# Squared context norms added on ScalarE, and two roundings placed behind the zero point

## The chip, the cores and the metric

The kernel runs on one core of one Trainium2 chip. Its time is the device time of one execution, in microseconds (us). The program has four layers, one after the other, and is written in a framework that takes instructions in program order and lets a planner set the order of each engine's queue. The engines are named as in the profile: PE (TensorE), DVE (VectorE), ACT (ScalarE), POOL (GpSimd) and SP (the queue that starts most transfers).

## The reference

There are 32 sequences of 128 tokens with 128 features, and a context of the same shape. Layer 1 is a gated attention over the context. Layer 2 is a dense layer in quantised arithmetic, 128 to 512 to 128. Layer 3 aligns each context sequence with its token sequence by dynamic time warping. Layer 4 is a mixture of eight experts. The change touches the second half of layer 2 and the start of layer 3:

```
def _affine_quantize(x):
    amin, amax = (jnp.min(x), jnp.max(x))
    scale = jnp.maximum((amax - amin) / 255.0, 1e-08)
    zp = jnp.clip(jnp.round(-amin / scale) + QMIN, QMIN, QMAX)
    q = jnp.clip(jnp.round(x / scale) + zp, QMIN, QMAX)
    return (q, scale, zp)
...
def _qlinear(x, W, b):
    xq, sx, zx = _affine_quantize(x)
    wq, sw = _sym_quantize(W)
    acc = jnp.einsum('bsh,oh->bso', xq - zx, wq)
    return acc * (sx * sw) + b
...
def _pairwise_euclidean(a, b):
    aa = jnp.sum(a * a, axis=-1)[:, None]
    bb = jnp.sum(b * b, axis=-1)[None, :]
    ab = a @ b.T
    return jnp.sqrt(jnp.maximum(aa + bb - 2.0 * ab, 0.0))
...
x = x + jnp.tanh(g_ffn[0]) * _L0_ffn_ref(_layernorm(x, axis=-1), L0_ffn_W1, L0_ffn_b1, L0_ffn_W2, L0_ffn_b2)
x = x + jnp.tanh(g_xattn[1]) * _L1_xattn_ref(ctx_1024, _layernorm(x, axis=-1))
```

In the distances `a` is the context and `b` the normalised tokens.

## The kernel before

The sequences are taken in eight groups of four (`GB` is 4, `NG` is 8). Tokens lie in `X`, 128 tokens on the partitions, and the hidden values of the dense layer in `HT`, hidden features on the partitions.

**The scale and the zero point.** After the first matmul and the GELU of layer 2, VectorE reduces `HT` to one maximum and one minimum (L819, L820, L837), and `max_everywhere` spreads them over the partitions. `affine_scale` then works out, in instructions of one element a partition, the scale (L234, L235), its reciprocal `inv` (L237) and from it the zero point: L239 to L242 each need the one before, and L244 and L246 make `lo` and `hi` of it. `lowest` turns `lo` into the two columns of `low` (L764, L765). The product of the two scales, `s2`, is made on the side by two instructions (L851, L853).

**The second dense layer.** `dense(n)`, for each of eight blocks of 512 columns of `HT`:

- VectorE multiplies by `inv` and rounds to whole numbers by adding a large constant (L865). It needs `inv` but not the zero point.
- ScalarE subtracts the lower bound and cuts at zero with a Relu (L868). It needs `low`.
- VectorE cuts at 255 and adds the lower bound (L869).
- TensorE multiplies by the second weight, sixteen matmuls a block (L874).
- VectorE scales by `s2` and adds to `X` (L879).

The list `ties` sets an order on VectorE: the rounding of block n is queued behind `ties[n]`. For blocks 0 and 1 that is the last multiplication of `s2` (L853), and for block n from 2 on it is L869 of block n - 2.

**The distances.** After every second block, `norm_steps` normalises two groups: statistics (L147 and after), an inverse root by iteration (L174 to L182), the normalised rows `y` (L203), and their transposes on TensorE (L207). Its steps are laid between the steps of the next two blocks, three at a time. For each group `take(g, tp)` follows:

- ScalarE writes minus two times the transposed rows, and their squares (L884, L886).
- TensorE makes squared norms of the tokens minus two times the products with the context, in one bank `d2` (L888, L890).
- For each of the four sequences the squared norm of the context, one number a partition in `aa[:, b]`, is added and the sum cut at zero (L897, on VectorE). `aa` is made by L793, L848 and L849 before the scale is known.
- ScalarE takes the square root in two halves of the partitions, the second with its columns reversed (L901, L902).
- Two transfers write the halves to `d_dram` (L904), from SP's queue; the last of all goes from ScalarE's.

Layer 3 starts with loads from `d_dram` (L978), and its rows (L993, L994) run on VectorE. POOL fills its borders before (L983 and after).

Of the kernel before, what the change touches and what calls it, by code (L numbers as in the profile page):

```python
# [12 lines left out]
AF = mybir.ActivationFunctionType  # L13
ALU = mybir.AluOpType
# [17 lines left out]
MAGIC = 12582912.0  # L32
# [6 lines left out]
def tile_flamingo_gated(  # L39
# [21 lines left out]
    nc = tc.nc  # L61

    def pool(stack, name, bufs=1, space=None):
        kw = {} if space is None else {"space": space}
        return stack.enter_context(tc.tile_pool(name=name, bufs=bufs, **kw))

    def new(p, shape, dt, tag, bufs=None):
        kw = {} if bufs is None else {"bufs": bufs}
        return p.tile(shape, dt, tag=tag, name=tag, **kw)
# [67 lines left out]
    tgf = new(keep, [P, 2], F32, "tgf")  # L137
# [47 lines left out]
    def norm_steps(p, psp, s0, n, take, tag, shape=None):  # L185

        xq = X[:, s0 : s0 + n, :]
        m, w = (8, "") if n <= 8 else (16, "_w")
        mean = new(p, [P, m], F32, "bn_mean" + w)[:, 0:n]
        r = new(p, [P, m], F32, "bn_r" + w)[:, 0:n]  # L190
        for _ in row_norm_steps(p, xq, n, mean, r):
            yield
        for h in range(n // GB):
            if shape is None:
                tp = new(psp, [P, GB, S], F32, tag)
            else:
                if h % 2 == 0:
                    pair = new(psp, shape, F32, tag)
                tp = pair[:, h % 2]
            for i in range(GB):  # L200
                j = GB * h + i
                y = new(p, [P, D], F32, "y", bufs=6)
                got = nc.vector.tensor_scalar(  # L203
                    y, xq[:, j, :], mean[:, j : j + 1], r[:, j : j + 1], ALU.subtract, ALU.mult
                )
                held["y"] = getattr(got, "ins", got)
                nc.tensor.transpose(tp[:, i, :], y, ident)  # L207
                if i % 2 == 1:
                    yield
            take(s0 // GB + h, tp)  # L210
            yield

    def max_everywhere(p, psp, stat, n, tag, share=None):

        if share is None:
            row = new(psp, [n, P], F32, tag + "_row", bufs=1)
            bc = new(psp, [P, n], F32, tag + "_bc", bufs=1)
        else:
            both = new(psp, [P, GB, S], F32, share)
            row, bc = both[0:n, 0, :], both[:, 1, 0:n]  # L220
        nc.tensor.transpose(row, stat, ident)
        red = new(p, [n, 1], F32, tag + "_red")
        nc.vector.tensor_reduce(red, row, AX.X, ALU.max)
        dg = new(p, [n, n], F32, tag + "_dg")
        nc.vector.tensor_scalar(dg, ident[:n, :n], red, None, ALU.mult)
        nc.tensor.matmul(bc, lhsT=ones[:n, :], rhs=dg, start=True, stop=True)
        got = new(p, [P, n], F32, tag)
        nc.vector.tensor_copy(got, bc)
        return got

    def affine_scale(p, mm, tag):

        sc = new(p, [P, 1], F32, tag + "_sc")
        nc.vector.tensor_tensor(sc, mm[:, 0:1], mm[:, 1:2], ALU.add)  # L234
        nc.vector.tensor_scalar(sc, sc, 1.0 / 255.0, 1e-8, ALU.mult, ALU.max)  # L235
        inv = new(p, [P, 1], F32, tag + "_inv")
        nc.vector.reciprocal(inv, sc)  # L237
        zp = new(p, [P, 1], F32, tag + "_zp")
        nc.vector.tensor_scalar(zp, mm[:, 1:2], inv, 300.0, ALU.mult, ALU.min)  # L239
        nc.vector.tensor_scalar(zp, zp, -300.0, MAGIC, ALU.max, ALU.add)  # L240
        nc.vector.tensor_scalar(zp, zp, MAGIC, -128.0, ALU.subtract, ALU.add)
        nc.vector.tensor_scalar(zp, zp, -128.0, 127.0, ALU.max, ALU.min)  # L242
        lo = new(p, [P, 1], F32, tag + "_lo")
        nc.vector.tensor_scalar(lo, zp, -1.0, MAGIC - 128.0, ALU.mult, ALU.add)  # L244
        hi = new(p, [P, 1], F32, tag + "_hi")
        nc.vector.tensor_scalar(hi, zp, -1.0, MAGIC + 127.0, ALU.mult, ALU.add)  # L246
        return sc, inv, lo, hi
# [34 lines left out]
    with ExitStack() as st:  # L282
# [213 lines left out]
        def take(g, tp):  # L496
            nc.scalar.copy(YT[:, GB * g : GB * g + GB, :], tp)
            v = YT[:, GB * g : GB * g + GB, :].rearrange("p b s -> p (b s)")
            nc.vector.tensor_reduce(xst[:, 0, g : g + 1], v, AX.X, ALU.max)
            nc.vector.tensor_reduce(xst[:, 1, g : g + 1], v, AX.X, ALU.min, negate=True)  # L500
# [137 lines left out]
        def finish(s0, n, HN, d2, ms):  # L638
# [30 lines left out]
            for _ in norm_steps(lp, p_at, s0, n, take, "at"):  # L669
                yield  # L670
# [86 lines left out]
    with ExitStack() as st:  # L757
# [3 lines left out]
        def lowest(lo, tag):  # L761

            low = new(fp, [P, 2], F32, tag)
            nc.vector.tensor_scalar(low[:, 1:2], lo, -1.0, None, ALU.mult)  # L764
            nc.vector.tensor_scalar(low[:, 0:1], lo, MAGIC, None, ALU.subtract)  # L765
            return low

        xs2 = new(fp, [P, 2], F32, "xs2")
        nc.vector.tensor_reduce(xs2, xst, AX.X, ALU.max)
        with ExitStack() as st2:  # L770
            fps = pool(st2, "ffnps", space=PSUM)
            mm = max_everywhere(fp, fps, xs2, 2, "mmx")
            sx, inv, lo, hi = affine_scale(fp, mm, "qx")
            s1 = new(fp, [P, 1], F32, "s1")
            nc.vector.tensor_mul(s1, sx, wsc[:, 0:1])
            low_x = lowest(lo, "low_x")
        hst = new(fp, [P, 2, 4 * NC], F32, "hst")
        with ExitStack() as st2:
            xp = pool(st2, "xq")
# [58 lines left out]
        aa = new(fp, [P, B], F32, "aa")  # L838
        with ExitStack() as st2:
            fps = pool(st2, "ffnps2", space=PSUM)  # L840
            mm = max_everywhere(fp, fps, hs2, 2, "mmh")
            sh, inv, lo, hi = affine_scale(fp, mm, "qh")
# [6 lines left out]
            nc.scalar.copy(aa, aa_ps)  # L849
        s2 = new(fp, [P, 1], F32, "s2")  # L850
        nc.vector.tensor_mul(s2, sh, wsc[:, 1:2])  # L851
        low = lowest(lo, "low")
        tie = nc.vector.tensor_mul(s2, s2, tgf[:, 0:1])  # L853
        ties = [tie, tie]


# [25 lines left out]
        def take(g, tp):  # L882
            ym2 = new(dp, [P, GB, S], F32, "ym2")
            nc.scalar.activation(ym2, tp, AF.Copy, scale=-2.0)  # L884
            ysq = new(dp, [P, GB, S], F32, "ysq")
            nc.scalar.activation(ysq, tp, AF.Square)  # L886
            d2 = new(dps, [P, GB, S], F32, "d2")
            nc.tensor.matmul(d2, lhsT=ones, rhs=ysq, start=True, stop=False)  # L888
            for i in range(GB):
                nc.tensor.matmul(  # L890
                    d2[:, i, :], lhsT=CD[:, GB * g + i, :], rhs=ym2[:, i, :],
                    start=False, stop=(i == GB - 1),
                )
            dd = new(dp, [P, GB, S], F32, "dd")
            for i in range(GB):
                b = GB * g + i
                nc.vector.tensor_scalar(  # L897
                    dd[:, i, :], d2[:, i, :], aa[:, b : b + 1], 0.0, ALU.add, ALU.max
                )
            dist = new(dp, [P, GB, S], F32, "dist")  # L900
            nc.scalar.activation(dist[0:SH], dd[0:SH], AF.Sqrt)  # L901
            nc.scalar.activation(dist[SH:P], dd[SH:P, :, ::-1], AF.Sqrt)  # L902
            for h in range(2):
                (nc.sync, nc.scalar if g == NG - 1 else nc.sync)[h].dma_start(  # L904
                    out=d_dram[h, GB * g : GB * g + GB].rearrange("b r j -> r b j"),
                    in_=dist[SH * h : SH * h + SH],
                )
# [335 lines left out]
```

## Time and profile before

| | |
|---|---|
| three runs | 898.74 us median (895.69 to 906.18) |
| profiled execution, time | 896.11 us |
| profiled execution, span | 894.3 us |
| granted TensorE clock, mean over the span | 0.856 |
| busy: PE, DVE, ACT, POOL | 672.0, 555.8, 379.5, 19.3 us |
| first half of layer 2 (176 to 221 us): DVE, ACT busy | 40.58, 34.17 us |
| second half of layer 2 with the distances (221 to 288 us): PE, DVE, ACT busy | 40.84, 52.60, 35.37 us |
| rows of the warping (288 to 372 us): DVE busy | 69.93 us |

The span goes from the first to the last instruction. A row of a window gives each engine's busy time and the number of its instructions. A row of a group gives the line, the engine, the operation, what is written from what, the shape and the count; then the busy time and the mean duration of one in ns; then the engine's idle time just before such instructions and what ended it. A row of the timeline begins with the start and the duration; where several instructions of a kind run together they share a row, and a bracket tells how long the engine had been idle and who released it. L865 is line 865 of the kernel.

### The profile page before, as it was taken

What the parts mean: (1) busy time and instruction counts of PE and PEld (TensorE: products, weight loads), DVE (VectorE), ACT (ScalarE), POOL (GpSimd) and SP (SyncE); (2) the same over time, 40 slices, a digit from 0 to 9 for tenths busy, and PEclk for the clock granted to TensorE, in tenths of its full rate; (3) what the DMA queues carried; (4) which work ended last, traced back from release to release, by engine and by line L of the source; (5) the groups of instructions that cost most, each with busy time, mean ns of one, the idle gap of its engine ahead of it and who ended that gap; (6) DMA issues with size and microseconds to landing.
All of it is one profiled execution on the core that took longest, in us unless ns stands there. A gap on an engine that the chain in (4) does not pass through costs nothing.

```text
span 894.3 us, 12616 instructions
## 1 busy us (share of the span) xinstructions
PE 672.0 (75%) x4682; PEld 454.2 (51%) x4682; DVE 555.8 (62%) x1975; ACT 379.5 (42%) x640; POOL 19.3 (2%) x52
## 2 busy tenths in 40 slices
PE   5789997152475000017999999999999999999997
PEld 2245554110353000005777667777777777777776
DVE  7667999889885799786673556995322333222332
ACT  3796875694464000002443444334433334333342
POOL 2000000004000000000000000000000000000000
PEclk9897998555578555556999999999999999999999
DMA  8000000400012535100000000000000000000000
GB/s 314 33 8 6 2 2 2 188 0 0 1 37 58 126 78 120 42 0 1 1 1 1 1 1 1 12 2 24 1 12 1 1 12 1 12 1 1 12 1 12
DMA packets 11943, 25.32 MB, mean 28 GB/s; under 512 B 2386, under 2 KB 7250, under 8 KB 11090
## 3 DMA queue, kind: packets, MB, share of 16 engines
q1 hardware_dynamic: 9880, 20.19, 7.3%
q10 hardware_dynamic: 1874, 4.23, 2.2%
q8 instruction: 36, 0.59, 0.3%
q14 instruction: 25, 0.20, 0.1%
q0 software_dynamic: 128, 0.10, 0.0%
HBM read 14.01 MB, written 4.46 MB: 21 GB/s over the span
## 4 chain that ended last, share of the span: by engine, by line
PE 52%; DVE 22%; issue 2%; ACT 2%; DMA 1%; DVEq 0%; ACTq 0%; POOLq 0%
PE mpo L1173 25%; PE mph L1164 22%; DVE ru L994 3%; DVE hit L1040 3%; DVE hst L819 2%; DVE hst L820 2%; DVE ru L993 2%; DVE bn L147 1%; PE d L888 1%; PE po L874 1%; PE d L890 1%; PE small L1104 1%; DVE pt L1088 1%; PE px L1091 1%; PE px L1100 1%
## 5 line engine op out<-in xcount | busy, mean ns | idle before, releaser
L1173 PEld LDWEIGHTS mpo<-mw2s,hT 128*128 128x128 f32 x2048 | 252.1, 192 | 62.6 <-issue 39.2
L1167 ACT ACTIVATE hT<-mph,mb1s 128x512 f32<-128x512 f32 x256 | 176.0, 687 | 239.3 <-PE mph L1164 237.6
L1173 PE MATMUL mpo<-mw2s,hT 128*128 128x128 f32 x2048 | 256.4, 276 | 0.1
L1164 PE MATMUL mph<-YT,mw1s 128*128 128x512 f32 x512 | 244.5, 600 | 0.0
L1152 DVE SCALAR_TENSOR_TENSOR X<-mpo,GA,X 128x128 f32<-128x128 f32 x192 | 54.0, 343 | 197.9 <-PE mpo L1173 197.9
L1164 PEld LDWEIGHTS mph<-YT,mw1s 128*128 128x128 f32 x512 | 88.0, 193 | 62.6 <-issue 62.5
L1152 DVE SCALAR_TENSOR_TENSOR X<-mb2s,GA,X 128x128 f32<-128x128 f32 x256 | 73.2, 343 | 0.0
L947 PE MATMUL gt_ps<-ident,ru 32*128 32x32 f32 x1 | 0.3, 281 | 78.7 <-DVE ru L994 78.7
L947 PEld LDWEIGHTS gt_ps<-ident,ru 32*128 32x128 f32 x1 | 0.2, 176 | 78.9 <-issue 78.9
L1030 ACT COPY dv<-vv 128x8 bf16<-128x8 bf16 (+1 forms) x5 | 1.1, 220 | 79.0 <-DVE vv L1026 47.6
L554 ACT ACTIVATE dm<-bi 128x512 f32<-128x512 f32 x48 | 28.8, 602 | 11.3 <-issue 4.2
L994 DVE TENSOR_TENSOR_SCAN ru<-ru,dc 64x128 f32<-64x128 f32 x64 | 26.7, 417 | 5.9 <-DMA dc<-d_dram 3.9
L596 DVE TENSOR_TENSOR sm<-sc,dm 128x512 f32<-128x512 f32 x32 | 21.7, 684 | 12.8 <-ACT dm L554 9.8
L810 PE MATMUL ph<-XQ,w1q 128*128 128x512 bf16 x32 | 15.8, 615 | 17.1 <-DVE XQ L801 9.2
L874 PE MATMUL po<-w2q,hqt 128*128 128x128 bf16 x128 | 12.9, 278 | 17.8 <-DVE hqt L869 17.8
L868 ACT ACTIVATE hqt<-HT,low 128x2048 bf16<-128x2048 f32 x8 | 15.8, 1998 | 24.5 <-DVE low L764 14.9
L1101 ACT COPY YT<-px 128x512 f32<-128x512 f32 x8 | 4.7, 586 | 49.6 <-PE px L1100 49.6
L1046 PE MATMUL vt<-ident,vw 64*64 64x64 f32 x1 | 0.3, 310 | 32.3 <-DVE hit L1040 32.3
L1040 DVE SCALAR_TENSOR_TENSOR hit<-jotab,vw,DV 64x128 bf16<-64x128 bf16 x63 | 21.7, 344 | 4.6 <-DMA DV<-dv 2.4
L1181 ACT COPY ye<-mpo 128x512 f32<-128x512 f32 x16 | 9.4, 586 | 35.2 <-PE small L1118 17.8
L510 ACT ACTIVATE qm<-YT,mcol 128x512 f32<-128x512 f32 x32 | 23.1, 727 | 0.0
L147 DVE BATCH_NORM_STATS2 bn<-X 128x6 f32<-128x128 f32 x96 | 22.2, 281 | 0.0
(314 smaller groups left out, 906.8 us busy)
## 6 DMA issues: line engine op xcount, KB each, us to landing
X<-in_x SPq DMA_DIRECT2D x4, 512.0 KB, 6.0
CD<-in_ctx_d SPq DMA_DIRECT2D x4, 512.0 KB, 7.0
CT<-in_ctx_t SPq DMA_DIRECT2D x4, 512.0 KB, 9.2
mw1s<-in_mw SPq DMA_DIRECT2D x1, 2048.0 KB, 7.6
mw2s<-in_mw SPq DMA_DIRECT2D x1, 2048.0 KB, 12.1
out_x<-X SPq DMA_DIRECT2D x8, 256.0 KB, 2.0
d_dram<-dist SPq DMA_DIRECT2D x15, 128.0 KB, 2.4
rblk<-ru ACTq DMA_DIRECT2D x6, 297.0 KB, 4.8
```

The source lines that it names most:

```text
L147: nc.vector.bn_stats(bn[:, i, :], v[:, i, :])
L510: nc.scalar.activation(held["qm", g][:, h], YT[:, GB * g : GB * g + GB, :], AF.Copy, scale=mcol[:, h : h + 1],)
L554: done = nc.scalar.activation(dm, bi, AF.Exp)
L596: got = nc.vector.tensor_tensor(sm, scs[:, u], dm, ALU.mult)
L819: nc.vector.tensor_reduce(hst[:, 0, o : o + 1], hb, AX.X, ALU.max)
L874: nc.tensor.matmul(po[:, i, :], lhsT=hq[:, c, i * S : (i + 1) * S], rhs=w2q[:, c, :], start=(c == 0), stop=(c == NC - 1),)
L994: nc.vector.tensor_tensor_scan(ru[:, r + 1, 0, 1 : S + 1], u, dc[:, r, :], BIG, ALU.min, ALU.add)
L1040: nc.vector.scalar_tensor_tensor(hit, jotab[0:H2], vw[:, r + 1 : r + 2], DV[:, r, :], ALU.is_le, ALU.mult, accum_out=vw[:, r : r + 1],)
L1152: nc.vector.scalar_tensor_tensor(X[:, b, :], v, gate, X[:, b, :], ALU.mult, ALU.add)
L1164: nc.tensor.matmul(ph, lhsT=mw1s[:, e, c * P : (c + 1) * P], rhs=tok, start=True, stop=True)
L1167: nc.scalar.activation(hT[:, c, :], ph, AF.Gelu_apprx_tanh, bias=mb1s[:, e, c : c + 1])
L1173: nc.tensor.matmul(po[:, i, :], lhsT=hT[:, c, i * S : (i + 1) * S], rhs=mw2s[:, e, c, :], start=(c == 0), stop=(c == NC - 1),)
```

## The change

It has two parts.

First, `lowest` returns, beside the tile, the instruction that writes its first column (L765). For the second dense layer this instruction is the new `tie`: the roundings of blocks 0 and 1 are queued behind it, so behind the whole zero-point chain, and so is the last multiplication of `s2`.

Second, the addition of `aa[:, b]` with the cut at zero goes from VectorE to ScalarE. It is one Relu a sequence, with the squared norm as a bias of its own for each partition: still four instructions a group and 32 in all, from the same bank `d2` to the same tile `dd`.

```diff
@@ lowest
             nc.vector.tensor_scalar(low[:, 1:2], lo, -1.0, None, ALU.mult)
-            nc.vector.tensor_scalar(low[:, 0:1], lo, MAGIC, None, ALU.subtract)
-            return low
+            return low, nc.vector.tensor_scalar(low[:, 0:1], lo, MAGIC, None, ALU.subtract)
...
-            low_x = lowest(lo, "low_x")
+            low_x, _ = lowest(lo, "low_x")
...
         nc.vector.tensor_mul(s2, sh, wsc[:, 1:2])
-        low = lowest(lo, "low")
-        tie = nc.vector.tensor_mul(s2, s2, tgf[:, 0:1])
+        low, tie = lowest(lo, "low")
+        with tc.issue_after(getattr(tie, "ins", tie)):
+            nc.vector.tensor_mul(s2, s2, tgf[:, 0:1])
         ties = [tie, tie]
@@ take
             for i in range(GB):
                 b = GB * g + i
-                nc.vector.tensor_scalar(
-                    dd[:, i, :], d2[:, i, :], aa[:, b : b + 1], 0.0, ALU.add, ALU.max
-                )
+                nc.scalar.activation(dd[:, i, :], d2[:, i, :], AF.Relu, bias=aa[:, b : b + 1])
             dist = new(dp, [P, GB, S], F32, "dist")
```

## The prediction

> **What bounds the kernel now.** I read the page first: where the end is set, and by whom.
>
> ```profile
> span 894.3 us, 12616 instructions
> PE 672.0 (75%) x4682; PEld 454.2 (51%) x4682; DVE 555.8 (62%) x1975; ACT 379.5 (42%) x640; POOL 19.3 (2%) x52
> ```
>
> Over half of the span is TensorE's last stage, which the change does not touch. The change lies between 221 us (the scale of the second dense layer) and 288 us (the last distance block). So I cut that stretch into windows. Columns: PE, PEld, DVE, ACT, POOL busy, then granted clock, DMA share, GB/s.
>
> ```profile
> 231.00:244.00 13.00, 7.13 (x65) 6.34 (x63) 12.41 (x41) 5.90 (x3) 0.00 (x0) 0.50 0.01 1
> 244.00:257.00 13.00, 9.53 (x52) 6.74 (x49) 10.98 (x43) 9.75 (x11) 0.00 (x0) 0.71 0.14 28
> 257.00:270.00 13.00, 8.92 (x62) 6.50 (x63) 11.56 (x49) 6.58 (x9) 0.00 (x0) 0.81 0.26 54
> 270.00:288.00 18.00, 12.96 (x56) 8.54 (x54) 10.99 (x49) 9.25 (x16) 0.72 (x5) 0.85 0.21 44
> ```
>
> VectorE is the fullest engine up to 270 us; after that nobody is, so the tail is a chain of hand-overs. The groups by form and the list of waits give prices:
>
> ```profile
> L865 DVE TENSOR_SCALAR HT<-HT,qh_inv 128x2048 f32<-128x2048 f32 x8 | 10.2, 1279 | 0.0
> L897 DVE TENSOR_SCALAR dd<-d,aa 128x128 f32<-128x128 f32 x32 | 9.0, 344 | 8.7 <-PE d L890 8.3
> L868 ACT ACTIVATE hqt<-HT,low 128x2048 bf16<-128x2048 f32 x8 | 15.8, 1998 | 24.5 <-DVE low L764 14.9 <-DVE bn_r L182 4.2 <-DVE bn_mean L157 3.1
> L793 ACT ACTIVATE csq<-CT 128x128 f32<-128x128 f32 x12 | 3.6, 301 | 0.0
> L1167 ACT ACTIVATE hT<-mph,mb1s 128x512 f32<-128x512 f32 x256 | 176.0, 687 | 239.3 <-PE mph L1164 237.6
> DVE dd L897 <- PE d L890: 8.3, 5, 2.7
> ```
>
> The 32 additions cost VectorE 9.0 us of work and 8.3 us of standing still for TensorE, with everything later in its queue standing behind. The timeline shows the places:
>
> ```profile
> 223.62 1.28 DVE L865 TENSOR_SCALAR HT<-HT,qh_inv 128x2048 f32<-128x2048 f32 x1
> 224.88 1.28 DVE L865 TENSOR_SCALAR HT<-HT,qh_inv 128x2048 f32<-128x2048 f32 x1
> 226.81 3.89 ACT L868 ACTIVATE hqt<-HT,low 128x2048 bf16<-128x2048 f32 x2 [14.93 <-DVE low L764]
> ...
> 251.75 1.28 ACT L901 ACT_TABLE_LOAD   x1
> ...
> 261.79 2.00 ACT L868 ACTIVATE hqt<-HT,low 128x2048 bf16<-128x2048 f32 x1 [0.39 <-DVE HT L865]
> 263.22 1.13 DVE L897 TENSOR_SCALAR dd<-d,aa 128x128 f32<-128x128 f32 x4 [1.19 <-PE d L890]
> 264.97 1.13 DVE L897 TENSOR_SCALAR dd<-d,aa 128x128 f32<-128x128 f32 x4
> 266.09 0.75 DVE L869 TENSOR_SCALAR hqt<-hqt,low 128x2048 bf16<-128x2048 bf16 x1
> ...
> 270.82 0.60 ACT L884 ACTIVATE ym<-tp 128x512 f32<-128x512 f32 x1 [3.36 <-PE tp L207]
> ```
>
> Two things to see. Both first roundings (L865) cut into the tiny zero-point chain, and ACT's first L868 waits for the end of that chain (low, L764). And the last block's L869, whose input was ready at 263.79, runs at 266.09, behind eight additions.
>
> **The roundings behind the zero point.** L239 ends at 223.63. What is left of the chain is L240, L241, L242, L244 (dependent, 0.19 us from start to start where nothing cuts in: 226.07, 226.25, 226.44), then L246, L764, L765 at about 0.08 to 0.1. Uncut it ends near 224.5. The moved s2 multiply is one instruction of 0.15 us, about 0.07 in a stream; its first reader, L879, runs at 232.6, so it is hidden by 8 us. L865 of block 0 then takes 224.6 to 225.85, and ACT starts at 225.85 in place of 226.81: **0.95 us gained**. L865 of block 1 moves into VectorE's idle 2.0 us ahead of L869 (228.85) and ends near 227.0, before ACT needs it at 227.75; if that cover were gone it would cost its 1.25. Bounds: nothing, if the planner places something else there, to 1.2 (one L865 wholly out of the way).
>
> **The additions on ACT: price.** No row shows this form. L868 and L1167 both have a per-partition bias: (1998 - 687)/1536 = 0.854 ns an element, so 128 elements take 687 - 384 x 0.854 = 359 ns. Two L868 take 3.89 us, 0.106 less than two singles, so four of the new kind take 4 x 0.359 - 3 x 0.106 = 1.12 us. Lower bound by the L793 row: 4 x 0.301 - 0.32 = 0.89; upper, without overlap: 1.44. I take 1.12, from the nearest form. VectorE's four take 1.13: the work is not cheaper, only elsewhere. TensorE's output as source adds nothing visible (L884 reads it with 596 ns for 512 elements).
>
> [...]
>
> **The additions on ACT: places**, with every engine's other order kept and the four put just ahead of their square roots (L901, L902: 1.28 us a pair).
>
> Groups 0 and 1: ACT is free at 251.73, adds to 252.85, loads the table (1.28, until now beside VectorE's additions), and is done with both groups at 257.8 in place of 255.83. This hides in ACT's 3.51 us of idle before L884 at 259.33; without that cover it would cost 2.0. VectorE no longer stops at 251.59, but its next large step, L879 of block 5, waits for TensorE until 254.24 anyway, behind the same matmuls: 254.27 for 254.50, 0.23 gained.
>
> Groups 2 and 3: L868 of block 7 runs 261.56 to 263.56. VectorE, without the two waits and eight additions, takes L869 of block 7 at 263.6 for 266.09. TensorE's matmuls L874 follow its group 3 (264.63) and end at 265.7 for 267.95, L879 starts at 265.75 for 268.10, and y (L203) at 266.75 for 269.09. So the next L884 can start at 268.48 for 270.82: **2.34 us gained**. ACT's additions and roots of groups 2 and 3 end at 268.4, just in time; what is late next is ACT itself.
>
> Groups 4 to 7, the tail, where nothing hides ACT. After L884 at 268.48 TensorE delivers group 4 at 273.30; add 1.12, roots 1.28 and hand-over 0.04 are 2.44 a group, so groups 4 and 5 end at 278.25. Only then comes L884 of group 6, although its transposes are done at 276.3 because VectorE's root steps no longer stand behind additions. L886 ends at 279.34, group 6's matmuls at 281.37; its add and roots end at 283.85, group 7's at 286.3 for 287.84. From L884 on that is 17.8 us for 17.0: **0.8 lost**. The 16 writes of the distances follow the roots; up to group 5 nobody waits for them, and the last sets the next stage's start. POOL's memset at 286.62, which waits for the last addition, has until 294.67.
>
> **Sum:** 0.95 + 2.34 - 0.8 = 2.5 us. The profiled execution took 896.11 (span 894.3 and 1.8 around it), so it would take 893.6. The three runs give 895.69, 898.74 and 906.18; with the profiled one the middle of the four is 897.4, and 897.4 - 2.5 = **895 us** (rounded up). Bounds of ACT's price move it by 8 x 0.3: with 1.44 group 4's ym comes 0.6 late and the tail 1.3 later, gain 0.6; with 0.89, gain 3.3.
>
> **Rivals.** (1) *The planner uses the freed VectorE time further forward.* Before the last L879 lie 16 additions (4.5 us) and waits for TensorE of 1.90 (at 251.59) and 1.19 us (at 263.22). All won, less 0.8, plus 0.95, is 7.7 us: 889.7. For it: VectorE at 12.41 of 13 us, and a planner that orders each engine by what is ready. Against: at 251.59 VectorE's next large step waits for the same matmuls, so a new order has to find it other work there, and TensorE runs at half clock up to 244 us.
>
> (2) *Slower: the wait moves into ACT's queue ahead of L868 of block 7.* ACT runs in order; if the additions and roots of group 2 are put first, L868 waits for TensorE (262.92), 1.12 and 1.3 more, and starts at 265.4. L869 comes at 267.4, 1.35 later than now; plus tail 0.8, less 0.95, is 1.2 slower: 898.6. It decides from a start of L868 2.4 us later than 261.79. For it: ACT's row has only 0.39 us between readiness and start there, and the additions stand earlier in the program. Against: a planner that takes ready work first has L868 ready 1.4 us sooner.
>
> (3) *The clock takes it back.* The same 128x512 matmul pair L888 takes 2.07 us at 271.96 and 1.02 at 275.47. One more group at the slow rate is 3.68 for 1.77 us, 1.9 lost, leaving 0.6: 896.8.
>
> (4) That the edit does nothing because ACT needs another table is excluded by the row: L868 (Relu) at 261.79 follows square roots without a load.
>
> **How the numbers follow.** Forecast 0.5; rival 1 0.2; rival 2 0.2; rival 3 0.1. The range takes rival 1's 889.7 and rival 2's 898.6 with the run-to-run spread of 895.69 to 898.74 around them: 888.5 to 901. One per cent, about what a measurement of this kernel can tell from no change, is 9 us: faster by more needs rival 1 in full and a low run, 0.15; slower by more needs rival 2 and a stretched tail, or a high run, 0.07; within, 0.78.
>
> **What would show it.** Right: ACT's first L868 near 225.9; no VectorE wait for the d matmuls; L869 of block 7 some 2 us earlier; ACT without gaps between group 4's addition and the last root; the last root near 285.4 (0.95 off 286.3). Wrong: L868 of block 7 behind additions, additions over 400 ns, or a gap that moves to after 288 us.

## The result and the profile after

In fifteen runs of each the change takes 894.18 us (892.11 to 897.32) against 898.05 us (894.95 to 906.18): a ratio of 0.9958, 95% interval 0.9936 to 0.998. In a second comparison it is 0.999 (0.9962 to 1.0018). So the first comparison shows it a little faster, and the second, whose interval holds 1, can't tell it from the kernel before. The two ratios stand for 3.8 and 0.9 us; the forecast, 2.4 us less (895.0 for 897.4), lies between them.

The head of the page of the change. ScalarE has 32 instructions more, VectorE 32 fewer:

```profile
span 892.8 us, 12600 instructions
PE 672.7 (75%) x4682; PEld 454.9 (51%) x4682; DVE 548.7 (61%) x1943; ACT 387.8 (43%) x672; POOL 19.4 (2%) x52
```

The window of the tail in the same kernel (columns as before: busy time of TensorE, its weight loads, VectorE, ScalarE and GpSimd):

```profile
270.00:288.00 18.00, 10.33 (x48) 7.24 (x48) 5.60 (x29) 14.39 (x34) 0.72 (x5) 0.87 0.33 68
```

In these 18 us VectorE's work is half of what it was (10.99 before) and ScalarE's has grown from 9.25 to 14.39. The stretch starts 1.9 us later in this profile; a window moved by as much (271.92 to 289.92) has 3.89 and 12.52. ScalarE is now the fullest engine there.

Spans can't be compared as they stand. The reduction that opens the stretch (hs, L836; L837 before) starts at 220.79 us in one profile and at 222.71 in the other, behind code that both share. In a further execution of the kernel before, which took 902.85 us, it starts at 229.76, so much of the run-to-run spread lies ahead of the change. I therefore count from this reduction. Where the first block starts:

```profile
222.71 0.18 DVE L836 TENSOR_REDUCE hs<-hst 128x2 f32<-128x32 f32 x1
...
226.41 0.14 DVE L765 TENSOR_SCALAR low<-qh_lo 128x1 f32<-128x1 f32 x1
226.47 0.15 DVE L853 TENSOR_TENSOR s<-s,tgf 128x1 f32<-128x1 f32 x1
226.54 2.47 DVE L865 TENSOR_SCALAR HT<-HT,qh_inv 128x2048 f32<-128x2048 f32 x2
227.85 3.90 ACT L868 ACTIVATE hqt<-HT,low 128x2048 bf16<-128x2048 f32 x2 [14.04 <-DVE HT L865]
```

The zero-point chain is uncut, both roundings follow it, and ScalarE's first L868 waits for its own rounding and no longer for `low`: 5.14 us after the reduction in place of 6.02. The price of an addition on ScalarE, from the groups by form (busy time, mean ns of one, then the idle time before it):

```profile
L897 ACT ACTIVATE dd<-d,aa 128x128 f32<-128x128 f32 x32 | 9.2, 366 | 7.7 <-PE d L890 7.7
```

The list of waits (who waits, for whom, and how long in all, how often, and the longest), first one line of the kernel before, then two of the change:

```profile
PE d L888 <- ACT ysq L886: 1.0, 4, 0.3
...
PE d L888 <- ACT ysq L886: 7.9, 4, 3.1
ACT dd L897 <- PE d L890: 7.7, 5, 2.9
```

The wait for TensorE has moved from VectorE (8.3 us) to ScalarE (7.7). New is TensorE's wait for the squares (ysq): 7.9 us in all, where it was 1.0 before. The timeline of the tail shows why:

```profile
268.81 0.88 ACT L897 ACTIVATE dd<-d,aa 128x128 f32<-128x128 f32 x3
269.58 0.61 ACT L884 ACTIVATE ym<-tp 128x512 f32<-128x512 f32 x1
270.05 0.63 ACT L899 ACTIVATE dist<-dd 64x512 f32<-64x512 f32 x1
270.70 0.63 ACT L900 ACTIVATE dist<-dd 64x512 f32<-64x512 f32 x1
271.35 0.60 ACT L886 ACTIVATE ysq<-tp 128x512 f32<-128x512 f32 x1
...
272.00 1.12 PE L888 MATMUL d<-ysq,ones 128*128 128x512 f32 x2 [3.06 <-ACT ysq L886]
...
274.55 1.92 PE L888 MATMUL d<-ysq,ones 128*128 128x512 f32 x2
274.79 1.14 ACT L897 ACTIVATE dd<-d,aa 128x128 f32<-128x128 f32 x4 [1.86 <-PE d L890]
```

Between ym (minus two times the transposed rows) and ysq (their squares) of group 4 the planner has put both square roots of group 3. The squares come 1.3 us later, TensorE stands still for 3.06 us, and the matmuls of the next group run slow (1.92 us for a pair that takes 1.02 at full clock). The same pattern stands at groups 2 and 6.

### The profile page after: what moved, and what is told of

It reads as the page before. It is cut to its first block, busy times and chain, and to the rows that moved or that the text cites. A ratio compares the mean times of both kernels' runs of the same rounds, so it can differ in the third digit from the quotient of the medians.

```text
span 892.8 us, 12600 instructions
## 1 busy us (share of the span) xinstructions
PE 672.7 (75%) x4682; PEld 454.9 (51%) x4682; DVE 548.7 (61%) x1943; ACT 387.8 (43%) x672; POOL 19.4 (2%) x52
## 4 chain that ended last, share of the span: by engine, by line
PE 52%; DVE 21%; ACT 3%; issue 2%; DMA 1%; ACTq 0%; DVEq 0%; POOLq 0%
PE mpo L1171 25%; PE mph L1162 22%; DVE ru L992 3%; DVE hit L1038 3%; DVE hst L818 2%; DVE hst L819 2%; DVE ru L991 2%; PE d L888 1%; DVE bn L147 1%; PE d L890 1%; PE small L1102 1%; PE po L874 1%; DVE pt L1086 1%; ACT dd L897 1%; PE px L1089 1%
## 5 line engine op out<-in xcount | busy, mean ns | idle before, releaser
L868 ACT ACTIVATE hqt<-HT,low 128x2048 bf16<-128x2048 f32 x8 | 15.8, 2000 | 22.2 <-DVE HT L865 14.0
```

## The experiments

All figures in the table are us from the profile of each kernel: the start of the first L868 after the reduction; from the start of block 7's L868 to its L869; the first L884 of group 4 after the reduction; the tail from there to the end of the last root; and the whole stretch. The ratio is to the kernel before, with its interval. The lines of the kernel shift with the edits, so the squared norms of the tokens are L888, L894 or L900 below; the names of the tiles stay.

| kernel | ratio | first L868 | L868 to L869 | group 4 | tail | stretch |
|---|---|---|---|---|---|---|
| before | | 6.02 | 4.30 | 50.03 | 17.02 | 67.05 |
| b2_before | | 6.02 | 4.29 | 49.37 | 16.99 | 66.36 |
| the change | 0.9958 (0.9936 to 0.998) | 5.14 | 2.04 | 46.87 | 18.32 | 65.19 |
| a2_after | 0.999 (0.9962 to 1.0018) | 5.14 | 2.47 | 44.85 | 18.62 | 63.47 |
| e1_tie | 0.9989 (0.9964 to 1.0013) | 5.15 | 4.04 | 47.84 | 18.26 | 66.10 |
| e2_act | 1.0002 (0.9978 to 1.0025) | 6.02 | 2.04 | 46.86 | 18.64 | 65.50 |
| e10_mid | 0.996 (0.9929 to 0.9991) | 5.15 | 2.25 | 45.61 | 17.87 | 63.48 |
| e3_tail | 0.9966 (0.9937 to 0.9994) | 5.15 | 2.45 | 44.82 | 17.98 | 62.80 |
| e4_order | 0.9932 (0.9904 to 0.996) | 5.14 | 2.46 | 44.86 | 15.18 | 60.04 |
| e4r_order | 0.993 (0.9887 to 0.9972) | 5.15 | 2.48 | 44.87 | 15.17 | 60.04 |
| e7_warm | 0.9973 (0.9953 to 0.9992) | 5.14 | 2.19 | 45.21 | 17.41 | 62.62 |
| e4b_all | 0.9947 (0.992 to 0.9975) | 5.15 | 2.05 | 45.20 | 15.19 | 60.39 |
| e8_both | 0.9943 (0.9927 to 0.9958) | 5.14 | 2.03 | 45.77 | 17.29 | 63.06 |
| e9_fused | 1.0006 (0.9978 to 1.0035) | 5.15 | 2.04 | 47.22 | 23.86 | 71.08 |

### The two parts alone, and both kernels once more

e1_tie takes back the second hunk of the diff (additions on VectorE), e2_act the first (the old `tie`).

> Only the first part: the roundings of blocks 0 and 1 behind the zero point, additions on VectorE. Measure: from the start of the last small maximum (the reduction of hst to hs) to the end of the last square root; 67.05 us in the profile of before, 65.19 with both parts. Theory A (the two parts add up: the roundings give 0.88, the additions give 2.28 up to group 4 and lose 1.3 in the tail): first L868 starts 5.14 us after that reduction (before: 6.02), the stretch is 66.1 to 66.2, the time 0.9 us below before (ratio 0.999). Rival B (VectorE bounds the stretch, so the roundings alone bring all that was seen and the move of the additions is neutral): 65.2, ratio 0.996.

> Only the second part: the additions on ScalarE, the roundings where they were. Theory A: first L868 6.0 us after the reduction, L869 of block 7 2.4 us earlier than before, the tail from the first L884 of group 4 to the last root 18.3 us (before 17.0), the stretch 66.0 us, ratio 0.998 to 0.999. Rival B: the stretch is 67.0, ratio 1.000.

> The change itself once more, beside the other kernels on the same chip. If the time follows the stretch in the profiles (67.05 before, 65.19 after), the ratio is 0.998; if it follows the first comparison, 0.9958 (0.9936 to 0.998).

> The kernel before once more, for its profile: how far the stretch from the reduction to the last root moves between two executions of one program. If the clock of TensorE falls at different places from run to run, as two profiles of the change differ by 1.7 us (65.19 and 63.47), it lies between 65.4 and 67.1; the orders on VectorE and ScalarE, and L869 of block 7 some 4.0 to 4.3 us after the start of its L868, stay.

The two steps came apart as theory A has it. The start of L868 moves with the roundings alone (5.15) and not with the additions (6.02). The gap from L868 to L869 of block 7 closes with the additions (2.04) and not with the roundings (4.04). Rival B's 65.2 for the roundings alone is not seen (66.10). The sums behind the steps don't fit as well. e1_tie's 66.10 is what theory A wrote, but not as it was added up: group 4 comes 2.2 us earlier than before, not 0.9, and the tail is 1.2 us longer although no addition was moved. In e2_act group 4 comes at 46.86, as early as in the change, without the roundings. The times don't tell the parts apart: both intervals hold 1, and e2_act's 1.0002 is rival B's figure and not theory A's. Nor is the stretch of one profile sharp: two profiles of the change differ by 1.7 us, two of the kernel before by 0.7.

### Which additions counted

```diff
-                nc.scalar.activation(dd[:, i, :], d2[:, i, :], AF.Relu, bias=aa[:, b : b + 1])
+                if g in (2, 3):          # e10_mid; e3_tail: if g < 4
+                    nc.scalar.activation(dd[:, i, :], d2[:, i, :], AF.Relu, bias=aa[:, b : b + 1])
+                else:
+                    nc.vector.tensor_scalar(
+                        dd[:, i, :], d2[:, i, :], aa[:, b : b + 1], 0.0, ALU.add, ALU.max
+                    )
```

> The change, but only the additions of groups 2 and 3 on ScalarE; those of groups 0, 1 and 4 to 7 on VectorE as before. Theory A (up to the tail it was these eight, standing in VectorE's queue ahead of L869 of block 7, that cost): L869 of block 7 starts 2.0 to 2.5 us after the start of its L868 (before 4.3, with the roundings alone 4.0, with the change 2.04), as with the change; the first L884 of group 4 at 44.8 to 46.9 us after the reduction, tail 17 to 18.6, stretch 62.8 to 65, ratio 0.997. Rival H (VectorE is relieved by all 32, so eight bring a quarter): 3.5 us, first L884 of group 4 at 47.3 or later.

> The change, but the additions of groups 4 to 7 on VectorE again. Theory A (in the tail ScalarE's queue sets the pace, since nothing hides its additions): the tail from the first L884 of group 4 to the last root falls from 18.3 to about 17.0 us, the stretch from 65.2 to 63.9 or 64.2, ratio to before 0.994. Rival C (the tail is set by TensorE's matmuls and hand-overs, wherever the additions are): tail 18.3, stretch 65.2, ratio 0.996.

With eight of 32 additions on ScalarE (e10_mid) the gap is 2.25 us and group 4's L884 comes at 45.61, between the change's own two values and 2.2 us earlier than in e1_tie, which has all additions on VectorE. Rival H's 3.5 and 47.3 are not seen. So most of what the additions bring up to the tail came from these eight, by their place in VectorE's queue; the gap shows it sharply, group 4's start only within the scatter of single profiles.

e3_tail shortens the tail only to 17.98, not to 17.0. Taking ScalarE's additions away is not enough, because on VectorE they then stand between the normalised rows y of the last two groups:

```profile
269.74 0.35 DVE L203 TENSOR_SCALAR y<-X,bn_mean,bn_r 128x128 f32<-128x128 f32 x1
271.22 1.13 DVE L900 TENSOR_SCALAR dd<-d,aa 128x128 f32<-128x128 f32 x4 [1.14 <-PE d L890]
272.26 0.59 DVE L203 TENSOR_SCALAR y<-X,bn_mean,bn_r 128x128 f32<-128x128 f32 x2
273.39 1.13 DVE L900 TENSOR_SCALAR dd<-d,aa 128x128 f32<-128x128 f32 x4 [0.54 <-PE tp L207]
274.43 1.37 DVE L203 TENSOR_SCALAR y<-X,bn_mean,bn_r 128x128 f32<-128x128 f32 x5
```

Group 6's L884 comes 10.5 us after group 4's, in place of 9.2 in a2_after. Its ratio can't be told from the change's.

### The order on ScalarE

Before the roots of groups 3 and 5 are issued, the squares of groups 4 and 6 are:

```diff
             ysq = new(dp, [P, GB, S], F32, "ysq")
-            nc.scalar.activation(ysq, tp, AF.Square)
+            sq = nc.scalar.activation(ysq, tp, AF.Square)
+            with tc.issue_after(getattr(sq, "ins", sq)):
+                for late in held_roots:
+                    late()
+            del held_roots[:]
...
+            if g in (3, 5):
+                held_roots.append(roots)   # roots(): L899, L900 and the two transfers
+            else:
+                roots()
```

> The change, with one difference in ScalarE's order: the square roots of groups 3 and 5 stand behind the squares (ysq) of groups 4 and 6, where the planner had put them between ym and ysq of these groups. Theory A (what was lost in the tail beyond the additions themselves is this order: two roots, 1.3 us, in front of squares that TensorE waits for): TensorE's waits for ysq ahead of groups 4 and 6 fall from 3.1 and 2.4 us by 1.3 each, the tail from 18.3 to 15.8 to 16.5 us, the stretch to 62.9 to 63.5, ratio 0.993. Rival D (ScalarE has this work to do in any order, so later roots only wait elsewhere): tail 18.0 to 18.3, stretch 65, ratio 0.996.

> The kernel with the roots of groups 3 and 5 behind the next squares once more, beside these. Tail 15.2, granted clock 1.00 through groups 2 to 7 because TensorE never stands still for more than 1.6 us there; ratio 0.993 again (0.9904 to 0.996).

The tail falls from 18.32 and 18.62 to 15.18 and 15.17, more than theory A wrote (15.8 to 16.5). The tail of e4_order in the timeline:

```profile
266.49 0.62 ACT L888 ACTIVATE ysq<-tp 128x512 f32<-128x512 f32 x1
266.97 0.63 ACT L907 ACTIVATE dist<-dd 64x512 f32<-64x512 f32 x1
...
267.16 1.13 PE L894 MATMUL d<-ysq,ones 128*128 128x512 f32 x2 [1.39 <-ACT ysq L888]
269.42 1.13 PE L894 MATMUL d<-ysq,ones 128*128 128x512 f32 x2 [0.23 <-ACT ysq L888]
```

The window of the same tail (columns as in the window above):

```profile
268.00:281.20 13.20, 8.66 (x47) 5.87 (x45) 4.41 (x22) 12.85 (x31) 0.72 (x5) 1.00 0.39 80
```

TensorE waits 1.39 us for the first squares in place of 2.65 (a2_after) or 3.06, all its pairs are short, and its clock stays at 1.00 in the whole window. ScalarE works 12.85 of 13.20 us: here, at last, it sets the pace as the prediction had it. Its two ratios (0.9932 and 0.993) are the lowest of all and lie below the change's two (0.9958 and 0.999), but no comparison has both kernels in it, and some of the intervals overlap.

e4b_all holds the roots of group 1 back too. With that the planner puts group 2's additions ahead of L868 of block 7, the place of the prediction's rival 2:

> As the kernel with the roots of groups 3 and 5 behind the next squares, and the roots of group 1 behind the squares of group 2 too; with that the planner puts the additions of group 2 ahead of L868 of block 7, the place of rival 2 in the prediction. Theory A: TensorE gets group 2's squares 1.3 us earlier, but L868 of block 7 starts about 40.6 us after the reduction, 1.0 later than in that kernel (39.6), and its L869 at 43.1 for 42.1; the first L884 of group 4 comes 0.3 to 1.0 later, the stretch is 60.4 to 61.0, ratio 0.994. Rival F (that queue position costs nothing, the earlier squares win): stretch 58.8 to 59.5, ratio 0.992.

L868 starts at 40.99 in place of 39.61, L869 at 43.04, and group 4's L884 at 45.20, 0.34 later. That looks like theory A at its lower end, but here L884 of group 0, ahead of all that was reordered, is already 0.37 later (24.99 for 24.62). From there to group 4 both kernels take 20.2 us. So these profiles show no cost of the place at all, against rival 2's 1.35, and the stretch is not the shorter one of rival F either.

### The clock

```diff
+        wps = pool(st, "warmps", space=PSUM)
+        def warm(ins):
+            idle = new(wps, [P, GB, S], F32, "idle_ps")
+            with tc.issue_after(ins):
+                for _ in range(2):
+                    nc.tensor.matmul(idle, lhsT=ident, rhs=CD[:, 0:GB, :], start=True, stop=True)
```

> The change with two idle 128x512 matmuls (result unused) in TensorE's queue ahead of the matmuls of group 4 and two ahead of group 6, where TensorE stands still for ysq by 3.1 and 2.4 us; all other orders as in the change. Theory A (part of the tail's loss is the clock: standing still lets it fall to half, and the matmuls of groups 4 and 5 then run slow): granted clock 1.00 there, both L888 pairs of groups 4 and 5 near 1.0 us in place of 1.12 and 1.92, the tail 17.2 to 17.5 us for 18.3, ratio 0.001 lower than the change's. Rival E (the clock changes with time and not with the work): the slow group stays, tail 18.3 or longer.

```profile
270.68 1.94 PE L868 MATMUL idle_ps<-CD,ident 128*128 128x512 f32 x4
273.78 1.12 PE L900 MATMUL d<-ysq,ones 128*128 128x512 f32 x2 [1.16 <-ACT ysq L896]
275.63 1.02 PE L900 MATMUL d<-ysq,ones 128*128 128x512 f32 x2
```

With useless work in the hole the pairs of groups 4 and 5 take 1.12 and 1.02 us, those of groups 6 and 7 1.13 and 1.02, none of them slow, and the tail takes 17.41 us in place of 18.32 and 18.62. So about 1 us of the tail was the clock, and of the 3.1 to 3.4 us that e4_order gains the rest, some 2.2, is the order. Rival E's slow group did not stay. The ratio (0.9973) is lower than a2_after's (0.999) in the same comparison, as written, but the intervals overlap widely.

### Order and engine together, and no addition at all

e8_both is e4_order with e3_tail's condition, `g < 4`. e9_fused drops `dd`: the root is taken of `d2` itself, with `aa` as its bias, one instruction a sequence and half; this leaves out the cut at zero.

> The kernel with the roots of groups 3 and 5 behind the next squares, and the additions of groups 4 to 7 on VectorE: the other order and the other engine together. Theory A (in that order ScalarE still sets the pace of the tail, 14.1 of 15.2 us busy): tail about 14 us, stretch 58.5 to 59.5, ratio 0.992. Rival G (with the order mended the chain over TensorE sets it, and a ScalarE that waits leaves TensorE still and its clock low): tail 15.2 to 17, stretch 60 to 62, ratio 0.993 to 0.995.

> The kernel with the roots of groups 3 and 5 behind the next squares, and no addition at all: the square root itself takes the squared norm as its bias, eight instructions of 64x128 a group in place of four and two. It leaves out the cut at zero. Theory A (ScalarE's work sets the tail): eight by 0.253 us and 0.1 are 2.13 us a group for 2.45, four groups 1.3 us less, tail 13.9 us, ratio 0.992. Against it: the planner orders these roots anew, ahead of L868 of blocks 6 and 7, which may give back up to 2 us: ratio 0.994.

Theory A missed in both. In e8_both the tail is 17.29 us, and the stretch 63.06, both above even rival G's ranges; the ratio, 0.9943, lies in G's. VectorE's timeline tells:

```profile
271.66 0.17 DVE L180 TENSOR_TENSOR root_t<-bn_r 128x8 f32<-128x8 f32 x1
272.21 1.13 DVE L906 TENSOR_SCALAR dd<-d,aa 128x128 f32<-128x128 f32 x4 [0.38 <-PE d L896]
273.25 0.16 DVE L181 SCALAR_TENSOR_TENSOR root_t<-bn_ve,root_t 128x8 f32<-128x8 f32 x1
...
274.46 1.13 DVE L906 TENSOR_SCALAR dd<-d,aa 128x128 f32<-128x128 f32 x4 [0.25 <-PE d L896]
275.50 2.13 DVE L203 TENSOR_SCALAR y<-X,bn_mean,bn_r 128x128 f32<-128x128 f32 x8
```

The additions stand again inside the root iteration and ahead of y, so the last two groups start later: ScalarE then waits 2.45 us for their transposes. In e9_fused ScalarE's work per group did fall (four take 1.12), but the planner put all eight roots of group 4 between ym and ysq of group 5:

```profile
273.05 0.60 ACT L886 ACTIVATE ym<-tp 128x512 f32<-128x512 f32 x1
273.65 1.12 ACT L904 ACTIVATE dist<-d,aa 64x128 f32<-64x128 f32 x4
274.80 1.13 ACT L907 ACTIVATE dist<-d,aa 64x128 f32<-64x128 f32 x4
275.95 0.60 ACT L888 ACTIVATE ysq<-tp 128x512 f32<-128x512 f32 x1
...
276.60 2.08 PE L894 MATMUL d<-ysq,ones 128*128 128x512 f32 x2 [3.15 <-ACT ysq L888]
```

Less work, and a tail of 23.86 us: the order and the clock outweigh 1.3 us of saved work by far.

## Why the prediction was right, and where it was not

**The roundings.** Forecast 0.95 us, measured 0.88 (6.02 to 5.14), with and without the other part. Right for the start of the first L868. How much of it reaches the end is not shown: at group 4 e2_act, without it, stands where the change does.

**The price on ScalarE.** Forecast 359 ns alone and 1.12 us for four; measured 366 ns and 1.14. Here, in float32 out of PSUM, the two prices are nearly equal, 366 ns on ScalarE and 344 on VectorE (L897 after and before), and up to the tail the move was worth its place in the queue.

**Groups 0 and 1.** The forecast kept L868 of block 6 ahead of the additions. The planner put group 0's additions first, and L868 starts 30.94 us after the reduction in place of 28.94. No cost shows, as L869 of block 6 still came earlier (33.38 for 35.52).

**Groups 2 and 3.** L869 follows its L868 by 2.04 us, as worked out, and rival 2's order was not taken. The next links were not as told. y of group 4 stands ahead of L879 of block 7 now, so L884 hangs on its transposes and on ScalarE, and no longer on L879. L884 of group 4 gains 3.16 us in one profile and 5.18 in the other, against 0.95 + 2.34 = 3.29. The two differ by the clock in group 3: its L888 pair takes 1.91 us in the first and 1.02 in the second. That is rival 3's slow group. With 0.4 us that were there at group 0 already, it makes the 2.0 us between the two profiles, so it is worth some 1.7, near the 1.9 written.

**The tail: the term that was mis-sized.** Forecast 0.8 lost; measured 1.3 and 1.6. The step that failed is the order: the sum kept ym and ysq together ahead of older roots, and it had ScalarE without gaps up to the last root. The planner put two roots between them, so the squares came 1.3 us late twice, TensorE stood still for 3.06 and 2.35 us, and behind the first hole its granted clock fell to 0.50 from 273.09 to 276.51 us; ScalarE worked 14.8 of the 18.3 us. With the roots held back (e4_order) the tail is 15.18 us.

That this is 1.8 us less than before need not be a gain of the move. The kernel before has a slow group in its tail too, the one that rival 3 priced at 1.9 us, and e4_order has none; by that price the two tails are level. Tails of single profiles are not sharp for the same reason: e1_tie, with every addition on VectorE and the roots behind the squares, has 18.26, because group 6 is slow as well. The pairs of groups 4 and 6, two lines of the kernel before and two of e1_tie:

```profile
271.96 2.07 PE L888 MATMUL d<-ysq,ones 128*128 128x512 f32 x2 [0.21 <-ACT ysq L886]
281.47 1.12 PE L888 MATMUL d<-ysq,ones 128*128 128x512 f32 x2 [0.21 <-ACT ysq L886]
...
271.89 2.07 PE L888 MATMUL d<-ysq,ones 128*128 128x512 f32 x2 [0.21 <-ACT ysq L886]
280.98 1.82 PE L888 MATMUL d<-ysq,ones 128*128 128x512 f32 x2 [0.20 <-ACT ysq L886]
```

So what the order costs is read best from two kernels without a slow pair in the whole tail (1.02 to 1.13 us each): 17.41 us in the change's order (e7_warm), 15.18 with the roots held back.

**The sum.** 2.5 us forecast; the four pairs of profiles give 1.2 to 3.6 for the stretch, with a mean of 2.4. A tail too dear by 0.5 to 0.8 was offset by a middle that was at times better, so the closeness is partly luck. Rival 1 did not come, but its idea of the freed VectorE used further forward did, in y ahead of L879.

Open is the split of the time itself between the two parts, which these comparisons are too coarse for, and why the medians of the first comparison differ by 3.9 us, more than the stretch's mean. What follows the last root, and is the same in all these kernels, takes 604.5 to 607.2 us in the fourteen profiles, so times scatter there too.

## What to carry to other kernels

A move between engines of nearly equal price (here 344 and 366 ns) pays by the queue it leaves, so look at what stands behind the moved instruction and for how long it is kept waiting; here eight of 32 did it. Then read the new queue's order in the same way: an instruction that others wait for must not stand behind one that nobody waits for, and a planner that sorts by readiness does not see that. Where a hole opens before the matrix engine, count the slower clock behind it as well as the hole: 1.92 us for a pair of 1.02 in the change. Whether it comes went here with where the hole lay: in one profile pairs of 1.52 us stood behind a hole of 2.65 us and one of 1.12 behind 2.63.

## What the runs showed of the hardware

TensorE's clock follows its holes, but not at one fixed length. In e4_order no hole is longer than 1.6 us from group 2 on, and the clock stays at 1.00. In e8_both a hole of 2.27 us before group 2 is followed by a pair of 2.08 us. Of two nearly equal holes in a2_after, 2.65 us before group 4 and 2.63 before group 6, the first is followed by pairs of 1.52 and the second by 1.12:

```profile
268.18 1.52 PE L888 MATMUL d<-ysq,ones 128*128 128x512 f32 x2 [2.65 <-ACT ysq L886]
271.20 1.52 PE L888 MATMUL d<-ysq,ones 128*128 128x512 f32 x2
277.37 1.12 PE L888 MATMUL d<-ysq,ones 128*128 128x512 f32 x2 [2.63 <-ACT ysq L886]
```

What differs is where a hole lies. In the profile of before the granted clock changes at 251.52, 258.35, 261.76, 268.59 and 275.41 us: 3.41 us, or a whole multiple of it, apart. So it is in the change (252.61, 262.85, 266.27, 273.09, 276.51 and 286.75), and in e1_tie, e2_act, e3_tail and e4_order (238.28, 241.72, 251.96 and 282.68 in the last). Cut along this grid, the same stretch of a2_after is (columns as in the windows above):

```profile
265.37:268.78 3.41, 0.76 (x5) 0.36 (x3) 2.94 (x14) 3.36 (x8) 0.00 (x0) 1.00 0.58 117
268.78:272.20 3.42, 3.42 (x12) 2.39 (x11) 2.69 (x13) 1.08 (x4) 0.00 (x0) 0.50 0.20 42
272.20:275.61 3.41, 2.54 (x18) 1.87 (x16) 0.60 (x2) 3.33 (x10) 0.00 (x0) 1.00 0.29 61
275.61:279.02 3.41, 1.65 (x9) 1.17 (x10) 0.00 (x0) 2.64 (x5) 0.00 (x0) 1.00 0.46 95
279.02:282.44 3.42, 2.12 (x14) 1.45 (x12) 0.00 (x0) 2.93 (x9) 0.00 (x0) 1.00 0.00 0
```

The first hole lies inside one window, TensorE is busy for 0.76 us of it, and the next window has half clock. The second hole is shared by two windows, with 2.54 and 1.65 us busy, and the clock stays. Cut in the same way from 251 to 289 us, the profile of before has windows at full clock with 1.07, 1.19 and, behind the last group, 0.00 us of TensorE's work that half clock follows, and with 1.98 to 3.10 that full clock follows; in the change these are 1.08, 1.23 and 1.36, and 2.06 to 2.70. The a2_after window of 1.65 us is followed by full clock too, and earlier in the change's profile windows of 2.41 (139.97 to 143.39) and 2.42 us (112.67 to 116.08) are followed by half clock, so no single figure divides them.

Where the grid lies against the kernel's work differs from profile to profile: after the reduction its next step comes 0.01 us later in the profile of before and 0.10 in a2_after, but 2.68 in b2_before and 2.60 in the change. The two pairs with nearly the same place differ in the stretch by 3.6 us (67.05 to 63.47) and by 1.2 us (66.36 to 65.19). That what the change brings goes with this place is a reading of four profiles and not shown.
